# An RWKV block on one core: a planned order of work, with side-by-side spreads, one pool of PSUM banks, regrouped mixes, a deviation by quarters and joint norm scalars

## The chip, the cores and the metric

The kernel runs on one core of a Trainium2 chip. The metric is the time of one execution in device microseconds (us); lower is better. A core has five engines that run side by side, each through its own instructions in order: TensorE (PE) for matrix products, VectorE (DVE), ScalarE (ACT) and GpSimd (POOL) for work on elements, and SyncE (SP), which here issues nearly all transfers (DMA). Each engine waits at an instruction until what it needs is there, and all that stands behind it on that engine waits too.

## The reference

All numbers are fp32: 8 sequences (batches), 256 tokens, 512 channels, 32 heads of 16 channels. Cut to what matters:

```python
xn = ln(x, ln1_w, ln1_b);  sx = shift(xn) - xn
xxx = tanh((xn + sx * maa_x) @ maa_w1).reshape(b, l, 5, 1, 32)
xxx = matmul(xxx, maa_w2)                          # five mix groups
x5 = xn[:, :, None] + sx[:, :, None] * (maa_stack + xxx)
w = exp(-exp(time_decay + tanh(x5[1] @ decay_w1) @ decay_w2))
r, k, v = x5[3] @ Wr.T, x5[0] @ Wk.T, x5[2] @ Wv.T
g = silu(x5[4] @ Wg.T)
def step(s, r, k, v, w):                           # per head, state s is 16 x 16
    a = k[:, None] * v[None, :]
    return a + w[:, None] * s, r @ (faaaa * a + s)
att = scan(step)                                   # over the 256 tokens
att = group_norm(att) * gn_w + gn_b                # over 16 channels of a head
x = x + att * g @ Wo.T
xn2 = ln(x, ln2_w, ln2_b)                          # a second shift and a gated FFN
x = x + sigmoid(xr @ ffn_Wr.T) * (square(relu(xk @ ffn_Wk.T)) @ ffn_Wv.T)
```

`x5[g]` stands for group g of the five; `xk` and `xr` are two more mixes of `xn2` with its shift.

## The kernel before, in words

Channels lie on the 128 partitions in four blocks; a tile of shape [128, 2, 256] holds two blocks (a half, q = 0 or 1) by 256 tokens. For each of the eight batches three stages are recorded.

`inputs_of_scan` (L588) loads x, norms it (`normed`, L491: statistics on DVE at L499 and L500, three small POOL instructions per tile of 128 tokens at L501 to L503, scaling on ACT at L505, transposition on PE at L517), forms the shift on POOL (L526) and the first mix (L537, L539), and makes the small product that feeds the five groups (L595, L582, tanh into the tile `ta`). `mixed` (L606) makes groups: a "lot" of four matmuls that contract over 32 rows each (L620), an add-and-multiply on DVE for each block (L629), an add on POOL (L631). It is called for groups (1, 0), then (2, 3), then (4,). Then come the decay (L582, L640, L650, L657) and the projections k, v, r and g (L552 and ACT copies at L665, L675).

`scan` (L677): for each of four blocks, v goes through DRAM (`vo`, issued by ACT at L712) and comes back four times as `vs`, repeated so that each partition has one of a head's 16 rows (the DMA recorded at L726). ACT writes the first column (L728), DVE multiplies by k (L731; `kp` is a copy of k in PSUM) and runs the recurrence as one scan of 1,024 elements (L733), POOL multiplies by r (L736). When four of these are done, PE sums over the rows (`gather`, L744, into the PSUM tile `pat`) and DVE adds the result to `att` (L750). The term with faaaa is formed once for each batch (L687, L692) as `c`, with one row for a group of channels, and is spread over the partitions by eight small DMAs for each half (`att<-c`, L705); POOL multiplies it by v (L707). DMAs that `dma` records all carry line 380 in the profile.

`rest` (L756): squares (L762), their mean over a head (L770, four matmuls into column strips of 32), square root (L775), reciprocal on DVE (L777, 256 elements wide). In seven batches the result is spread by eight small DMAs for each half (L799) and POOL multiplies (L801); in the last, PE spreads it (L785) and DVE multiplies (L793). Then the scale of the group norm (L805), the product with g (L807), the output product (`project_tokens`, L567), the second norm, and the FFN with its three products (L552, L567). The weights Wo, ffn_Wk, ffn_Wr and ffn_Wv are loaded anew for each batch into eight tiles `Ws`.

The order of all instructions is made when the program is built, by the class `Plan`. Each piece of work is recorded with its engine, a cost in us, what it writes and what it reads. `TURNS` gives each piece a rank (a list written out by hand, one number for each piece of each stage). `order` (L281) takes pieces that can start, lowest rank first, gives them a start time from the recorded costs, latencies and free buffers, and the program is emitted by start time. Buffers come from named pools; a piece takes a buffer when it is placed, and the buffer comes free when the last piece that names it is done. The costs in the plan are therefore part of what sets the order. In PSUM there are eight banks: two for `wrep`, two for `kp`, one for `pat`, three for `ps` (all other products). `mix` has eight tiles, `vs` five.

The recorder lets a piece that writes a tile wait for the last writer and all readers of that tile. In the plan, the eight spreads into one tile are therefore one after the other, each with the recorded DMA latency:

```python
LATENCY = {"PE": 0.25, "DVE": 0.12, "ACT": 0.2, "POOL": 0.15, "DMA": 2.6}
def dma(out, in_, dst, kb, src=None):
    plan.add("DMA", 0.05 + kb / 300, ...)
```

Of the kernel before, what the change touches and what calls it, by code (L numbers as in the profile page):

```python
# [12 lines left out]
P = 128  # L13
# [18 lines left out]
C_SUM = C_MEAN + 32  # L32
# [4 lines left out]
class Buf:  # L37


    def __init__(self, pool, name, view=lambda t: t):  # L40
        self.pool, self.name, self.place, self.left, self.view = pool, name, None, 0, view
        self.writer, self.readers, self.until = None, [], 0.0
        self.first = self.last = None
# [14 lines left out]
class Plan:  # L58
# [4 lines left out]
    LATENCY = {"PE": 0.25, "DVE": 0.12, "ACT": 0.2, "POOL": 0.15, "DMA": 2.6}  # L63
    SWITCH = {"ACT": 1.3, "PE": 0.1}

# [12 lines left out]
    def add(self, engine, us, outs, ins, emit, mode=None, into=(), lag=0.0):  # L78
        op = Op(engine, us, outs, ins, emit, mode)
        op.lag = self.LATENCY[engine] + lag  # L80
# [4 lines left out]
        for b in ins:  # L85
            edges.add(b.writer)
            b.readers.append(op)
        for b in outs:
            edges.add(b.writer)
            edges.update(b.readers)  # L90
            b.writer, b.readers = op, []
        for o in edges - {None, op}:
            op.before.append(o)
            o.after.append(op)
        self.stages[-1].append(op)

    def stage(self):
# [6 lines left out]
        388 1540 181 998 1450 2523 1312 1981 2661 297 2571 1221 1131 2433 2751 711 2162 4536 2071 1620 2857 3167  # L104
        3186 3205 414 621 531 440 207 971 1019 1205 1064 1112 1459 1157 1376 1668 1283 1331 1401,
        0 90 350 420 450 472 530 564 441 510 549 571 629 663 822 973 991 1047 1119 767 847 865 921 993 1263 1311
        1375 1113 1161 1225 1495 1681 1931 1971 2000 2359 2481 2524 2576 2564 2607 3421 2055 2177 2257 2309 2217
        2297 2681 2706 2826 2855 2883 2912 3106 3228 3803 3272 3510 3575 3921 4119 5076 5252 5450 2576 2698 2777
        2863 2738 2817 2968 2879 3001 3044 3096 3084 3127 3201 3226 3402 3600 3748 4440 4869 4094 4613 4811 4267
        4786 4984 4969 5164 5365 5416 5124 5204 5256 6788 7016 7298 6109 6285 6630,  # L110
        817 908 1168 1237 1579 1601 1659 1726 1258 1328 1480 1502 1560 1594 1830 2025 2044 2111 3526 2194 2274 2292
        2348 2420 3711 3759 3823 2540 3848 5127 5425 5611 5731 5771 5799 6468 6602 6802 7476 6642 6842 6957 5855
        5977 6057 6226 6017 6338 6852 7816 7975 8004 8033 8082 9245 9367 9414 9759 9806 8137 8313 8595 7189 7545
        7917 8005 8178 8258 8536 8218 8298 8746 7438 7674 7754 8058 7714 7914 8641 8713 8889 9087 10184 10711 10909
        9525 9701 9899 9062 9352 9550 9884 10076 10500 10552 10036 10236 10405 11001 11177 12506 11874 12120 12448,
        1710 1891 2060 2130 2786 2808 3325 3359 2337 2407 3306 3344 3402 3436 6961 7227 7245 7356 8430 5962 6089
        6127 6183 7062 8551 8653 10300 7182 7408 8851 10420 10606 10726 10765 10794 11360 11732 11812 12909 11532
        11692 11798 10894 11148 11268 11693 11109 11228 11480 13203 13499 13528 13557 13585 14239 14361 14408 14453
        15185 12329 12505 12703 12795 12971 13184 12688 13101 13181 13252 13061 13141 13412 13308 13485 13685 13920
        13445 13524 13576 14056 14346 14751 14519 14695 14893 15260 15436 15634 13707 13883 14081 15120 15303 15567  # L120
        16084 15263 15951 16266 16386 16562 16946 17149 17325 17651,
# [818 lines left out]
```

## Time and profile before

| what | value |
|---|---|
| three timed runs | 699.48, 701.94, 705.77 us; median 701.94 |
| the profiled execution | 702.79 us, of it a span of 701.0 |
| granted TensorE clock, mean | 0.978 |
| busy: PE, DVE, POOL, ACT | 649.5, 570.3, 539.2, 347.0 us |
| DMA | 132.09 MB, mean 188 GB/s |
| scan on DVE (L733), 128 times | 2278 ns each |
| multiply by k on DVE (L731), 128 times | 1206 ns each |
| multiply by r on POOL (L736), 128 times | 2000 ns each |
| reciprocal on DVE (L777), 8 times | 1743 ns each |
| first `vs` multiply; last gather's end | 48.25 us; 647.0 us |
| `vs<-vo`, issue to landing, median | 5.6 us, 512 KB read out each |
| `att<-c`, `rk<-sq`, `sq<-sq`, issue to landing | 4.0, 4.0 and 3.7 us |

How to read it: a row of the costliest groups gives line, engine, operation, what is written and read with sizes, the count, busy us and mean ns, and then the idle time of that engine just before those instructions with what ended it. `PE ... x8` counts records: an fp32 matmul leaves two. PE's busy time counts a matmul that runs at a lower granted clock as longer. Releasers are inferred. A wait of an engine costs time only where that engine, or what waits for it, sets the end.

### The profile page before, as it was taken

Reading aid. Unit: us, or ns where it says so; the run is one execution under the profiler, and the core shown is the slowest. Engines: PE = TensorE matmul, PEld = TensorE weight load, DVE = VectorE, ACT = ScalarE, POOL = GpSimd, SP = SyncE. Lnnn points to the kernel's source line nnn. Section 1 sums busy time; section 2 is a strip of 40 time slices with the busy share of each in tenths; the row PEclk is TensorE's granted clock in tenths of the full one; section 3 lists DMA queues with packets and bytes.
Section 4 is the critical chain, followed back from the end, with each engine's and each line's share of the span. In section 5 each row is a group of like instructions: output and inputs, shape, how many; then the busy total and the mean of one; then the engine's idle time right before and its main releaser. Section 6 shows DMA issues by size and latency. Waiting matters only on the chain.

```text
span 701.0 us, 10714 instructions
## 1 busy us (share of the span) xinstructions
PE 649.5 (93%) x3688; PEld 429.8 (61%) x3688; DVE 570.3 (81%) x567; ACT 347.0 (50%) x716; POOL 539.2 (77%) x474
## 2 busy tenths in 40 slices
PE   5799999899899899999999999999999999698997
PEld 4487676675646486557764686577756676345453
DVE  2539999999999999889898889899797999896310
ACT  5244542543882467425582368246753365463450
POOL 4528789688898998688978799698877988679151
PEclk9699999999999999999999999999999999999999
DMA  8778754757879669865987669968787658983442
GB/s 269 229 184 212 170 137 114 188 147 189 206 198 243 181 144 243 216 184 162 237 217 198 179 177 230 242 174 222 180 210 181 161 157 200 233 226 114 142 152 89
DMA packets 65415, 132.09 MB, mean 188 GB/s; under 512 B 11281, under 2 KB 24081, under 8 KB 65361
## 3 DMA queue, kind: packets, MB, share of 16 engines
q1 hardware_dynamic: 60752, 127.21, 69.8%
q10 hardware_dynamic: 4608, 4.20, 2.0%
q8 instruction: 29, 0.48, 0.3%
q14 instruction: 26, 0.20, 0.1%
HBM read 115.11 MB, written 8.39 MB: 176 GB/s over the span
## 4 chain that ended last, share of the span: by engine, by line
PE 39%; DVE 11%; DMA 10%; issue 5%; ACT 2%; POOL 2%; SPq 2%; POOLq 0%; DVEq 0%; ACTq 0%
PE ps L567 15%; PE ps L552 14%; DMA vs<-vo 7%; DVE st L733 5%; PE pat L744 4%; DVE vs L731 3%; PE ps L620 3%; SPq L380 2%; DMA att<-c 1%; PE ps L582 1%; DMA s<-in_state 1%; DMA Ws<-in_wo 1%; PE ps L517 1%; PE ps L595 1%; DVE mix L629 1%
## 5 line engine op out<-in xcount | busy, mean ns | idle before, releaser
L733 DVE TENSOR_TENSOR_SCAN st<-wrep,vs 128x1024 f32<-128x1024 f32 x128 | 289.5, 2278 | 7.8 <-PE pat L744 2.6
L736 POOL TENSOR_TENSOR st<-st,r 128x1024 f32<-128x1024 f32 x128 | 255.1, 2000 | 43.1 <-DVE st L733 32.7
L731 DVE TENSOR_TENSOR vs<-vs,kp 128x1024 f32<-128x1024 f32 x128 | 152.9, 1206 | 20.5 <-ACT vs L728 20.3
L567 PE MATMUL ps<-Ws,mix 128*128 128x512 f32 x256 | 119.1, 612 | 6.7 <-DMA Ws<-in_fr 4.3
L631 POOL TENSOR_TENSOR mix<-mix,xn 128x512 f32<-128x512 f32 x80 | 86.5, 1090 | 32.0 <-DVE mix L629 31.8
L728 ACT ACTIVATE vs<-s,cm 128x4 f32<-128x4 f32 x128 | 36.8, 296 | 116.7 <-DMA vs<-vo 113.6
L567 PEld LDWEIGHTS ps<-Ws,mix 128*128 128x128 f32 x256 | 48.3, 195 | 64.5 <-issue 56.4
L629 DVE SCALAR_TENSOR_TENSOR mix<-ps,vec,sx 128x256 f32<-128x256 f32 x160 | 67.8, 474 | 12.6 <-PE ps L620 11.6
L744 PE MATMUL pat<-st,con 128*32 128x256 f32 x1024 | 64.0, 386 | 6.0 <-DVE att L750 5.8
L552 PE MATMUL ps<-mix,Wg 128*128 128x256 f32 x256 | 62.9, 397 | 0.9 <-DVE mix L629 0.9
L552 PE MATMUL ps<-mix,Ws 128*128 128x256 f32 x256 | 58.0, 382 | 4.6 <-ACT vs L728 1.9
L552 PE MATMUL ps<-mix,Wv 128*128 128x256 f32 x256 | 61.7, 392 | 0.0
L552 PE MATMUL ps<-mix,Wk 128*128 128x256 f32 x256 | 59.9, 384 | 1.4 <-ACT sq L775 0.8
L552 PE MATMUL ps<-mix,Wr 128*128 128x256 f32 x256 | 59.2, 382 | 1.2 <-POOL mix L631 0.8
L552 PEld LDWEIGHTS ps<-mix,Wg 128*128 128x128 f32 x256 | 49.0, 197 | 14.8 <-issue 5.0
L567 PE MATMUL ps<-Ws,g 128*128 128x512 f32 x128 | 56.9, 596 | 0.7 <-POOL g L807 0.7
L552 PEld LDWEIGHTS ps<-mix,Ws 128*128 128x128 f32 x256 | 47.9, 190 | 13.6 <-POOL mix L539 4.9
L539 POOL TENSOR_TENSOR mix<-mix,xn 128x512 f32<-128x512 f32 x48 | 51.6, 1091 | 5.9 <-ACT mix L537 5.7
L552 PEld LDWEIGHTS ps<-mix,Wk 128*128 128x128 f32 x256 | 47.6, 190 | 13.2 <-issue 4.6
L552 PEld LDWEIGHTS ps<-mix,Wv 128*128 128x128 f32 x256 | 48.7, 195 | 10.7 <-issue 3.2
L552 PEld LDWEIGHTS ps<-mix,Wr 128*128 128x128 f32 x256 | 47.9, 190 | 10.4 <-issue 1.9
L744 PEld LDWEIGHTS pat<-st,con 128*32 128x32 f32 x1024 | 31.1, 110 | 34.9 <-DVE att L750 9.4
(82 smaller groups left out, 815.4 us busy)
## 6 DMA issues: line engine op xcount, KB each, us to landing
vs<-vo SPq DMA_DIRECT2D x128, 512.0 KB, 5.6
Ws<-in_wo SPq DMA_DIRECT2D x32, 256.0 KB, 5.0
Ws<-in_fv SPq DMA_DIRECT2D x32, 256.0 KB, 4.0
Ws<-in_fk SPq DMA_DIRECT2D x32, 256.0 KB, 4.0
Ws<-in_fr SPq DMA_DIRECT2D x32, 256.0 KB, 4.7
xt<-in_x SPq DMA_DIRECT2D x16, 256.0 KB, 3.1
x<-in_x SPq DMA_DIRECT2D x16, 256.0 KB, 5.0
vo<-v ACTq DMA_DIRECT2D x32, 128.0 KB, 3.8
```

The source lines that it names most:

```text
L380: plan.add("DMA", 0.05 + kb / 300, [out] if out else [], [src] if src else [], lambda: nc.sync.dma_start(out=dst(), in_=in_()))
L539: gp(512, t, [t, xn[q]], lambda q=q, t=t: nc.gpsimd.tensor_tensor(t(), t(), xn[q]()[:, :, 1 : T + 1], ALU.add), 1.8)
L552: nc.tensor.matmul(ps()[:, m, :], lhsT=w[k]()[:, o : o + P], rhs=src[k // 2]()[:, k % 2, :], start=(k == 0), stop=(k == NK - 1),)
L567: nc.tensor.matmul(ps().rearrange("p m t -> p (m t)"), lhsT=src[h]()[:, k % 2, n * P : (n + 1) * P], rhs=w[k](), start=(k == 0), stop=(k = ...
L620: nc.tensor.matmul(ps[g, q]()[:, m, :], lhsT=w2()[lo : lo + MAA, k * P : (k + 1) * P], rhs=ta()[lo : lo + MAA, i, :], start=True, stop=True,)
L629: dve(256, [t], [p_, vec, sx[q]], lambda g=g, q=q, m=m, t=t, p_=p_: nc.vector.scalar_tensor_tensor(t()[:, m, :], p_()[:, m, :], col(f"maa_ ...
L631: gp(512, t, [t, xn[q]], lambda q=q, t=t: nc.gpsimd.tensor_tensor(t(), t(), xn[q]()[:, :, 1 : T + 1], ALU.add), 1.8)
L728: act(4, vs, [s0, cm], lambda i=i, blk=blk, vs=vs: nc.scalar.activation(vs()[:, :, 0:1], s0()[:, blk, 4 * i : 4 * i + 4].rearrange("p (n o ...
L731: dve(4 * T, [vs], [vs, kp], lambda m=m, vs=vs, kp=kp: nc.vector.tensor_tensor(vs(), vs(), kp()[:, m : m + 1, :].to_broadcast([P, 4, T]), ...
L733: dve(4 * T, [st], [w, vs], lambda w=w, vs=vs, st=st: nc.vector.tensor_tensor_scan(st().rearrange("p n t -> p (n t)"), w().rearrange("p n ...
L736: gp(4 * T, st, [st, r], lambda m=m, st=st, r=r: nc.gpsimd.tensor_tensor(st(), st(), r()[:, m : m + 1, :].to_broadcast([P, 4, T]), ALU.mult))
L744: nc.tensor.matmul(pat()[32 * i : 32 * i + 32, 0, :], lhsT=con()[:, s : s + 32], rhs=done[i]()[:, j, :], start=(j == 0), stop=(j == 3),)
```

## The change

Seven things are changed together.

- In the plan, the parts of a spread (pieces that write parts of one tile) no longer wait for each other (`part=True`); a tile keeps a list of writers.
- The plan's prices: an issued DMA holds SP for 0.6 and then a shared wire for kb/270; the latencies, a gap between dependent pieces of one engine (`GAP`), and the costs of ACT, DVE and POOL pieces have other numbers.
- PSUM: `kp`, `pat` and `ps` become one pool of six banks. `mix` has 12 tiles instead of 8, `vs` 6 instead of 5. A setting of the program (`dynamic_dma_scratch_size=1024`) is added.
- `mixed` is called for groups (1, 0, 2) and (3, 4): lots of six and of four matmuls.
- In all batches but the last, the mean of squares is laid out by quarters of the tokens: sixteen matmuls of 64 columns fill all 128 rows of a tile 64 wide. Square root and reciprocal run on 64 elements, one DMA writes the result to DRAM (`dev`), and the spreads read it from there.
- The norm's scalars of both token tiles are made together: two POOL instructions and one DVE instruction for a norm, in place of six on POOL.
- L707 and L807 have their operands the other way round, and all of `TURNS` is new.

```diff
-    LATENCY = {"PE": 0.25, "DVE": 0.12, "ACT": 0.2, "POOL": 0.15, "DMA": 2.6}
+    LATENCY = {"PE": 0.3, "DVE": 0.18, "ACT": 0.16, "POOL": 0.12, "DMA": 1.1}
+    GAP = {"PE": 0.03, "DVE": 0.16, "ACT": 0.04, "POOL": 0.11, "DMA": 0.03}
...
-            edges.add(b.writer)
-            edges.update(b.readers)
-            b.writer, b.readers = op, []
+            if not part or b.readers or not b.writers or b.writers[0].engine != engine:
+                b.before = {*b.writers, *b.readers}
+                b.writers, b.readers = [], []
+            edges.update(b.before)
+            b.writers.append(op)
...
-            free[op.engine] = op.end
+            free[op.engine] = landed = op.end
+            if op.wire:
+                wire = landed = max(wire, op.end) + op.wire
...
-        plan.add("DMA", 0.05 + kb / 300, [out] if out else [], [src] if src else [], lambda: nc.sync.dma_start(out=dst(), in_=in_()))
+        plan.add("DMA", 0.6, [out] if out else [], [src] if src else [], lambda: nc.sync.dma_start(out=dst(), in_=in_()),
+                 lag=lag, kb=kb, part=part)
...
-    pool("mix", 8, [P, 2, T])
+    pool("mix", 12, [P, 2, T])
...
+    pool("dev", 2, [H, T], dram)
-    pool("vs", 5, [P, 4, T])
+    pool("vs", 6, [P, 4, T])
...
-    pool("kp", 2, [P, 2, T], pp)
-    pool("pat", 1, [P, 2, T], pp)
-    pool("ps", 3, [P, 2, T], pp)
+    pool("ps", 6, [P, 2, T], pp)
...
-            gp(1, rs, [mv, eh], each=60, emit=lambda rs=rs, mv=mv: nc.gpsimd.tensor_tensor(rs(), mv()[:, 1:2], eh()[:, 0:1], ALU.add))
-            gp(1, rs, [rs, eh], lambda rs=rs: nc.gpsimd.tensor_tensor(rs(), rs(), eh()[:, 1:2], ALU.pow), 420)
-            gp(1, nm, [mv, rs], lambda nm=nm, mv=mv, rs=rs: nc.gpsimd.tensor_scalar(
-                nm(), mv()[:, 0:1], rs(), -1.0, ALU.mult, ALU.mult), 60)
+        gp(2, rs, [mv, eh], lambda: nc.gpsimd.tensor_tensor(rs(), mv()[:, :, 1], eh()[:, 0:2], ALU.add), 30)
+        gp(2, rs, [rs, eh], lambda: nc.gpsimd.tensor_tensor(rs(), rs(), eh()[:, 2:4], ALU.pow), 250)
+        dve(2, [nm], [mv, rs], lambda: nc.vector.scalar_tensor_tensor(
+            nm(), mv()[:, :, 0], -1.0, rs(), ALU.mult, ALU.mult))
...
-            if len(pair) == 2:
-                lots = [[(pair[0], q, w2a, pair[0], 0), (pair[1], q, w2a, pair[1], 0)] for q in range(NQ)]
-            else:
-                lots = [[(4, q, w2b, q, 1) for q in range(NQ)]]
+            lots = [[(g, q, w2b, 0, 1) if g == 4 else (g, q, w2a, g, 0) for g in pair] for q in range(NQ)]
...
-        x5 = mixed((1, 0))
+        x5 = mixed((1, 0, 2))
...
-        x5.update(mixed((2, 3)))
+        x5.update(mixed((3, 4)))
...
-        x5.update(mixed((4,)))
...
-                    att(), att(), v()[:, :, 1 : T + 1], ALU.mult), 1.85)
+                    att(), v()[:, :, 1 : T + 1], att(), ALU.mult))
...
+        parts = 1 if b == NB - 1 else 4
+        nt, c = T // parts, C_MEAN if parts == 1 else C_QUA
...
+                for i in range(parts):
+                    at = blk % 2 * T + nt * i
+                    nc.tensor.matmul(
+                        pv()[32 * blk : 32 * blk + 32, 0, 0:nt], lhsT=con()[:, c + 32 * i : c + 32 * i + 32],
+                        rhs=sqs[blk // 2]()[:, at : at + nt], start=(i == 0), stop=(i == parts - 1))
...
+        dve(nt, [rs], [rs], lambda: nc.vector.reciprocal(rs()[:, 0:nt], rs()[:, 0:nt]), 6.25)
+        if parts > 1:
+            dev = new("dev", f"dev{b}")
+            dma(dev, lambda: rs()[:, 0:nt], lambda: dev().rearrange("h (u t) -> (h u) t", u=parts), 32, rs, 0.8)
...
-                        dma(rsb, lambda blk=2 * q + n: rs()[32 * blk : 32 * blk + 32, 0:T],
-                            lambda n=n, rows=rows, rsb=rsb: by_block(rsb)[rows, n, :], 32, rs)
+                        dma(rsb, lambda blk=2 * q + n: dev()[HB * blk : HB * blk + HB, :].unsqueeze(1).to_broadcast([HB, 4, T]),
+                            lambda n=n, rows=rows, rsb=rsb: by_block(rsb)[rows, n, :], 32, dev, 0.8, True)
...
-            gp(512, g, [g, att], lambda g=g, att=att: nc.gpsimd.tensor_tensor(g(), g(), att(), ALU.mult))
+            gp(512, g, [g, att], lambda g=g, att=att: nc.gpsimd.tensor_tensor(g(), att(), g(), ALU.mult))
```

In the changed kernel the lines of the prediction's steps stand at L590 (mix lots), L700 and L702 (multiply and scan), L713 (gather), L743 (mean of squares), L750 (reciprocal), and DMAs at L351.

## The prediction, made before the result

> **What bounds the kernel now.** I read the page first, then a table of stretches, the waits by engine, and the chain of waits in order of time.
>
> ```profile
> span 701.0 us, 10714 instructions
> PE 649.5 (93%) x3688; PEld 429.8 (61%) x3688; DVE 570.3 (81%) x567; ACT 347.0 (50%) x716; POOL 539.2 (77%) x474
> PE   5799999899899899999999999999999999698997
> DVE  2539999999999999889898889899797999896310
> PEclk9699999999999999999999999999999999999999
> ```
>
> PE is the fullest engine, but DVE stands at 9 through the first third. The table of stretches shows the two limits apart (busy us of PE, PEld, DVE, ACT, POOL; granted clock; DMA share):
>
> ```profile
> 20.00:30.00 10.00, 6.50 (x38) 4.21 (x36) 6.87 (x17) 1.55 (x4) 5.51 (x7) 0.57 0.98 319
> 30.00:40.00 10.00, 8.92 (x31) 6.47 (x32) 3.88 (x8) 3.67 (x9) 6.89 (x10) 0.58 0.23 67
> 180.00:200.00 20.00, 17.31 (x119) 12.10 (x118) 19.52 (x17) 17.91 (x40) 18.73 (x16) 1.00 0.86 225
> 400.00:420.00 20.00, 20.00 (x122) 16.43 (x115) 16.67 (x16) 12.25 (x28) 16.57 (x17) 1.00 0.62 167
> 580.00:600.00 20.00, 15.59 (x89) 11.38 (x88) 17.75 (x11) 10.23 (x20) 14.99 (x11) 1.00 0.86 217
> 600.00:620.00 20.00, 16.09 (x65) 8.64 (x66) 16.93 (x13) 9.21 (x16) 14.04 (x10) 0.83 0.90 212
> ```
>
> From 20 to 40 us PE waits and then runs at 0.57 of its clock. From 50 to 280 us DVE is busy for 220.4 of 230, and PE waits for it. From 280 to 580 PE is full and DVE waits. From 580 to 620 both wait: 8.3 us of PE idle, and 3.4 us (20 x 0.17) to a lower clock. After 647 only PE's closing work is left.
>
> ```profile
> ACT vs L728 <- DMA vs<-vo: 113.6, 50, 6.2
> DVE vs L731 <- ACT vs L728: 20.3, 13, 5.6
> PE ps L567 <- DMA Ws<-in_fr: 4.3, 1, 4.3
> SPq L380 <- DVE st L733: 96.1, 45, 5.9
> ```
>
> The scan's inputs (vs) come by DMA through a free vs buffer; ACT puts in the first column and DVE follows. DVE loses 20.3 us there, and the 4.3 us of PE in the 580 stretch is a weight load that was issued late, among spreads.
>
> ```profile
> 397.09 1.73 PE ps L552 x8
> 398.82 1.06 PE ps L620 x8
> 399.88 1.86 PE pat L744 x32
> 401.75 1.93 PE ps L552 x8
> ```
>
> This piece of the chain prices PE: eight records (four matmuls of 256 columns) take 1.73 us, and 0.20 more when PE comes from another tiling (pat) to them; a lot of four 32-row matmuls (L620) takes 1.06; sixteen 32-column matmuls, four side by side, 1.86.
>
> **The sum's base.** The profiled execution took 702.79 us (span 701.0 and 1.8 around it), 0.85 above the median 701.94. I change 702.8 and take 0.85 off.
>
> **Mix groups three and two.** 40 lots of L620 become 32; the 160 matmuls stay, 16 lots hold three groups and 16 two. If the third row group runs beside the others as the fourth column group does in L744, a lot stays at 1.06: 8 x 1.06 = 8.5 us off PE. If only two run side by side, a lot of three costs 0.43 more: 16 x 0.43 gives 6.8 back, 1.6 off. I take -7.8, near the first, because L744 is the row with more than two side by side.
>
> **Deviation by quarters.** The matmuls of line 770 (eight records in 0.64 us at 512.28) become 32 records of 64 columns for seven batches. They are written block by block, so four in a row go to the same column strip. Least: 0.64, as now, the same columns in all. Most: the sixteen-record, 128-column row of L582 (1.02 us, 0.064 a record) gives 32 x 0.064 = 2.05. I take 1.0 more each, +7 (0 to +9.9). On DVE the reciprocal (1.743 us, L777) runs on a quarter of the elements: 0.44 to 0.5, seven times, -8.7. On ACT the square root gets shorter, which hides. On SP, seven more DMAs, and the spreads must now wait until the copy in DRAM has landed: the small spreads land in 3.8 us (median), vo in DRAM also in 3.8, and SP issues one in 0.59. In six of the seven batches the first spread stands right behind that copy in SP's order, so all behind it, vs loads and weights, wait too.
>
> The Trainium skill, "TensorEngine Tiling", section Performance Considerations, speaks against the quarters: a matmul carries about 60 cycles of overhead, and a dimension that is already small should not be tiled further. No row here has 64 columns; an estimate from that page puts the price at the upper end, 2.9 us of PE more than I take, of which 1.8 would fall in the PE-bound part: a forecast near 686.
>
> **PE's changes of tiling.** In the two built orders they go from 177 to 163: 14 x 0.19 = -2.7. PE in all: -7.8 + 7 - 2.7 = -3.5 (-11.2 to +5.6).
>
> **Joint norm scalars.** Each norm drops six POOL instructions (2 x (189 + 549 + 265) ns = 2.0 us) for two (0.19, and 0.55 to 1.1 for the power), and gives DVE one small instruction, 0.18 by L500: POOL loses 0.7 to 1.3 a norm, about 16 in all, under DVE's and PE's cover; DVE 16 x 0.18 = +2.9. Both tiles must now be in before either is scaled; that costs only where no other matmul is queued, the tail. Swapping the operands of L707 and L807 can change POOL by 0.18 and 0.09 each against the 1.09 us of its kin, 16 times: -4.4 to +4.4, covered by DVE and PE as the rest.
>
> **Six shared banks, 12 mix, 6 vs buffers; new turns.** The order moves all engines' instructions, but not the balance: summed over my rows, PE's work ahead of the 16th gather is the same within 2 us, ahead of the 28th 3 us less. So I cost the new order by stage.
>
> Head: at 22.91 the second lot waits 2.54 us for DVE to empty a bank, the third 0.96, then 1.08 more at 33.02; all at the low clock. Six banks let the first six groups go in one piece. DVE needs 12 x 0.415 = 5.0 us for them and POOL 6 x 1.09, so v can start some 4 us earlier than at 35.03, and with it the first scan (48.25). SP's loads before the first vs are 36 as against 42. -4 (0 to -7, if the copies of x that stand ahead of vs on SP come as late as now, or not).
>
> DVE-bound, 48 to 280: three reciprocals 3.7 less, five norms 0.9 more: -2.8. Of the 9.6 us of DVE idle here the sixth vs buffer and the free pat bank take a quarter: -2.2. Together -5 (0 to -12).
>
> PE-bound, 280 to 640: five eighths of -3.5: -2 (-7 to +3.5). PE idle and clock loss from 280 to 620 are 13.9 + 5.2 = 19.1 us (the clock: 1.8 at 0.91 from 360 to 380, 3.4 from 600), 11.7 of it the stretch from 580 to 620, where SP issues two dozen spreads one by one between vs and weight loads. The planner now prices such an issue at 0.6, near its row (0.59; it had 0.16), so a plan made by it should not walk into that. I take less than half, -8 (0, if new stalls of that size come, to -18). What comes late next is vs behind a run of spreads.
>
> Tail, after the last gather: 40 token matmuls as before, one more fk group of 1.73 to fill; the joint scalars wait for the second tile (0.69 + 0.69), and the two matmuls left after the transposes cover 1.7 us where four covered 3.5: +1 (0 to +3).
>
> Sum: -4 - 5 - 2 - 8 + 1 = -18: 702.8 - 18 = 684.8, less 0.85: 684 us.
>
> **Rivals.** Slower: SP. In the after order the longest runs of other DMAs between two vs loads are 21, 21, 21, 19 and 19; before 17, 17, 15 and 14 (the loads at the start left out). 21 x 0.59 + 3.8 of standing = 16.2 us. Six vs buffers last 6 x (1.21 + 2.28) = 20.9 us of scan, less 5.6 for the next landing: 15.3. It is short by 0.9 where DVE has only scan work. If the copy lands at the upper end of its rows (6.0, so 2.2 later) and the next vs 1.2 above its median (its rows reach 12.3), it is short by 4.3: seven batches, 30 us, 714 us. It decides from 3.6 us a batch ((709 - 684)/7). For it: 113.6 us of ACT's waits are for vs. Against it: DVE has other work between scans (570 us for 128 scans is 4.5 us each, not 3.5), which stretches the cover by 6 us.
>
> The Trainium skill, "DMA: Bandwidth & Descriptors", section Anatomy of one DMA, puts about 2.0 us of fixed time on a DMA of the software path, most of it the receipt from the target memory, heaviest for HBM. Our vo row has 3.8 on a hardware queue, and the measurement decides; with 2.0 the run would last 14.4 and this rival would vanish, the forecast staying at 684.
>
> No change: the edits do what they say on paper, but the third group does not run beside the others, the quarters cost the most, and the new turns have stalls as large as the old: five eighths of 9.1 and the 8 come back: 684 + 6 + 8 = 698. For it: the balance of the order hardly moves. Against: 8.3 us of PE's idle stands in one stretch with one cause, spreads priced too low in the plan.
>
> More gain: banks and vs buffers end most waits between 48 and 640: -12 in the DVE part, -18 in the PE part: 684 - 7 - 10 = 667. Against: full buffers only help where a buffer was the last to come.
>
> **How the numbers follow.** Forecast 0.46 (671 to 695), more gain 0.17, no change 0.18, SP 0.19. Measuring this kernel cannot tell less than about 1% (7 us) from nothing. Faster 0.63, within 1% 0.18, slower 0.19. The range 664 to 712 leaves out the better half of the best case and the worse half of the SP case; the likeliest case alone has 671 to 695.
>
> **What would show it.** Right: line 590's lots of three at about 1.1 us; DVE reciprocals near 0.5; the first scan before 46 us; no stretch after 50 us with more than 3 us of PE idle in 20; granted clock over 0.98. Wrong: line 743 over 1.7 us a batch; DVE waiting for ACT vs over 25 us in all, behind SP waiting for dev; PE idle of 8 us in one stretch.

## The result, and the profile after

The changed kernel takes 723.22 us (median; 719.36 to 724.22), the kernel before 702.64 us on the same chip: a ratio of 1.028, interval [1.023, 1.033]. It is slower by 2.8%; 684 us were forecast, with 712 as the upper end. The profiled execution of the changed kernel took 719.36 us, its span is 717.6, 16.6 us over the span before.

The page of the changed kernel, its busy times, slices and the chain by engine and by line:

```profile
span 717.6 us, 11006 instructions
PE 646.2 (90%) x3856; PEld 432.9 (60%) x3856; DVE 570.1 (79%) x583; ACT 345.5 (48%) x718; POOL 518.2 (72%) x410
PE   5899799988998898999989999998899898879987
PEclk9999999999999999999999999999999999989999
PE 29%; DMA 18%; DVE 14%; issue 8%; ACT 7%; SPq 6%; POOL 4%; ACTq 1%; POOLq 0%; DVEq 0%
```

PE has 3.3 us less to do than before and still ends 16.6 later: its idle time rose from 51.5 to 71.4 us. SP's queue holds 6% of the chain; it held 2%. The table of stretches (columns as in the prediction):

```profile
20.00:30.00 10.00, 7.76 (x52) 5.74 (x47) 7.81 (x21) 5.02 (x12) 8.52 (x10) 0.83 0.86 303
30.00:40.00 10.00, 10.00 (x53) 8.03 (x53) 5.49 (x12) 5.72 (x13) 7.02 (x7) 1.00 0.61 157
580.00:600.00 20.00, 19.40 (x147) 15.92 (x146) 15.94 (x13) 11.35 (x25) 13.28 (x11) 1.00 0.89 199
600.00:620.00 20.00, 17.30 (x87) 12.02 (x86) 17.00 (x11) 10.66 (x21) 16.34 (x11) 0.91 0.76 194
620.00:640.00 20.00, 13.61 (x54) 5.78 (x53) 15.99 (x13) 10.57 (x16) 13.59 (x9) 0.83 0.68 168
```

The head is better, as meant: no slow clock from 30 to 40 us. The hole of 580 to 620 has moved to 600 to 640. The waits, of all engines and then of SP's own queue (in one execution: total us, times, longest us):

```profile
DVE vs L700 <- ACT vs L697: 29.7, 22, 4.6
DVE nm L474 <- POOL rs L473: 9.7, 9, 1.6
PE ps L540 <- DMA Ws<-in_wo: 6.2, 3, 3.4
PE ps L540 <- DMA Ws<-in_fv: 3.9, 2, 3.0
PE ps L540 <- DMA Ws<-in_fr: 2.3, 1, 2.3
```

```profile
SPq L351 <- DVE st L702: 86.5, 34, 9.1
SPq L351 <- DMA vo<-v: 63.8, 12, 9.9
SPq L351 <- DMA dev<-sq: 23.4, 6, 5.1
```

DVE waits 9.4 us more for vs than before, PE 12.4 us for weights in these rows (before: 4.3 + 1.1), and SP has a new row: 23.4 us behind the copy to DRAM. The timeline of SP in the fourth batch shows that row as it comes about:

```profile
355.98 0.55 SPq L351 DMA_DIRECT2D vs<-vo  x1
356.62 0.53 SPq L351 DMA_DIRECT2D dev<-sq  x1
361.01 1.43 SPq L351 DMA_DIRECT2D rk<-dev  x2
...
373.01 0.66 SPq L351 DMA_DIRECT2D rk<-dev  x1
373.77 0.39 SPq L351 DMA_DIRECT2D Ws<-in_fv  x1
374.27 2.48 SPq L351 DMA_DIRECT2D vs<-vo  x4
```

The copy is issued at 356.62, the first spread at 361.01, the last ends at 373.67: SP is taken for 17.1 us, 4.4 of it from the copy's issue to the first spread, and a spread takes 0.65 to 0.7 us to issue (0.59 before). Four vs loads and the last part of ffn_Wv wait behind.

Where the time went can be read from the start of the first scan of each batch in DVE's timeline, and of the last scan of all (one execution each, in us):

| kernel | batch 0 | 1 | 2 | 3 | 4 | 5 | 6 | 7 | last scan | end |
|---|---|---|---|---|---|---|---|---|---|---|
| before | 49.5 | 118.1 | 189.5 | 260.9 | 342.0 | 418.4 | 498.8 | 575.6 | 638.5 | 701.0 |
| after | 41.5 | 111.6 | 183.1 | 259.4 | 340.4 | 422.9 | 508.4 | 591.4 | 654.4 | 717.6 |
| after, without the copy (e1_direct) | 43.1 | 111.9 | 181.4 | 254.6 | 336.1 | 416.1 | 498.2 | 574.3 | 634.9 | 696.4 |

The change gains 8.0 us in the head, keeps 6.4 of it to batch 2, and then loses 22 us from batch 2 to the last scan. The tail loses 0.7.

### The profile page after: what moved, and what is told of

Its sections match the earlier page's. It is cut to its first block, busy times and chain, and to the rows that moved or that the text cites. A ratio compares the mean times of both kernels' runs of the same rounds, so it can differ in the third digit from the quotient of the medians.

```text
span 717.6 us, 11006 instructions
## 1 busy us (share of the span) xinstructions
PE 646.2 (90%) x3856; PEld 432.9 (60%) x3856; DVE 570.1 (79%) x583; ACT 345.5 (48%) x718; POOL 518.2 (72%) x410
## 4 chain that ended last, share of the span: by engine, by line
PE 29%; DMA 18%; DVE 14%; issue 8%; ACT 7%; SPq 6%; POOL 4%; ACTq 1%; POOLq 0%; DVEq 0%
PE ps L540 14%; DMA vs<-vo 11%; PE ps L525 8%; DVE st L702 7%; SPq L351 6%; DVE vs L700 4%; PE ps L713 3%; DMA Ws<-in_wo 2%; DMA att<-c 2%; PE ps L590 1%; DVE mix L599 1%; ACT mix L510 1%; DMA dev<-sq 1%; POOL st L705 1%; ACT xh L478 1%
## 5 line engine op out<-in xcount | busy, mean ns | idle before, releaser
L702 DVE TENSOR_TENSOR_SCAN st<-wrep,vs 128x1024 f32<-128x1024 f32 x128 | 288.7, 2280 | 12.7 <-ACT wrep L687 5.7
L700 DVE TENSOR_TENSOR vs<-vs,ps 128x1024 f32<-128x1024 f32 x128 | 152.6, 1209 | 30.1 <-ACT vs L697 29.7
L540 PE MATMUL ps<-Ws,g 128*128 128x512 f32 x128 | 63.3, 649 | 14.5 <-POOL g L783 8.2
L713 PE MATMUL ps<-st,con 128*32 128x256 f32 x1024 | 66.3, 397 | 7.4 <-POOL st L705 4.6
L599 DVE SCALAR_TENSOR_TENSOR mix<-ps,vec,sx 128x256 f32<-128x256 f32 x160 | 65.5, 477 | 9.2 <-PE ps L590 9.1
L525 PE MATMUL ps<-mix,Ws 128*128 128x256 f32 x256 | 59.8, 389 | 4.2 <-POOL mix L512 3.9
L525 PE MATMUL ps<-mix,Wg 128*128 128x256 f32 x256 | 59.2, 384 | 3.0 <-ACT mix L798 2.8
L525 PEld LDWEIGHTS ps<-mix,Wv 128*128 128x128 f32 x256 | 49.5, 197 | 10.0 <-issue 2.3
L713 PEld LDWEIGHTS ps<-st,con 128*32 128x32 f32 x1024 | 32.2, 113 | 38.4 <-issue 11.9
L540 PEld LDWEIGHTS ps<-Ws,g 128*128 128x128 f32 x128 | 25.8, 206 | 48.1 <-issue 32.5
```

The costliest lines, as they stand in the source:

```text
L525: nc.tensor.matmul(ps()[:, m, :], lhsT=w[k]()[:, o : o + P], rhs=src[k // 2]()[:, k % 2, :], start=(k == 0), stop=(k == NK - 1),)
L540: nc.tensor.matmul(ps().rearrange("p m t -> p (m t)"), lhsT=src[h]()[:, k % 2, n * P : (n + 1) * P], rhs=w[k](), start=(k == 0), stop=(k = ...
L599: dve(256, [t], [p_, vec, sx[q]], lambda g=g, q=q, m=m, t=t, p_=p_: nc.vector.scalar_tensor_tensor(t()[:, m, :], p_()[:, m, :], col(f"maa_ ...
L700: dve(4 * T, [vs], [vs, kp], lambda m=m, vs=vs, kp=kp: nc.vector.tensor_tensor(vs(), vs(), kp()[:, m : m + 1, :].to_broadcast([P, 4, T]), ...
L702: dve(4 * T, [st], [w, vs], lambda w=w, vs=vs, st=st: nc.vector.tensor_tensor_scan(st().rearrange("p n t -> p (n t)"), w().rearrange("p n ...
L713: nc.tensor.matmul(pat()[32 * i : 32 * i + 32, 0, :], lhsT=con()[:, s : s + 32], rhs=done[i]()[:, j, :], start=(j == 0), stop=(j == 3),)
```

## The experiments

All ratios are to the kernel before on the same chip, with their 95% intervals. Theories at the start: S, SP's standing for the copy costs the time; N, DVE's new wait for POOL's power does; T, the new turns do.

**Without the copy.** e1_direct: the deviation runs 256 wide and the spreads read it from SBUF, as before; turns and order stay.

```diff
-        parts = 1 if b == NB - 1 else 4
+        parts, spread = 1, b < NB - 1
...
-            dma(dev, lambda: rs()[:, 0:nt], lambda: dev().rearrange(...), 32, rs, 0.8)
...
-            dma(rsb, lambda blk=2 * q + n: dev()[HB * blk : HB * blk + HB, :].unsqueeze(1).to_broadcast([HB, 4, T]),
+            dma(rsb, lambda blk=2 * q + n: dev()[32 * blk : 32 * blk + 32, :],
```

> The after kernel with its own turns and the same order on every engine; only the deviation goes back to full width (four matmuls, a reciprocal of 256 elements) and the spreads read it from SBUF, without the copy to DRAM. SP no longer stands for the copy (23.4 us in six waits in the after trace), DVE has 7 x 1.2 = 8.5 us more work, PE 7 x 0.68 = 4.8 us less. Theory S, the stand on SP is the cause: vs and weights come earlier, DVE and PE stalls shrink, 705 to 714 us. Theory T, the new turns follow a plan that the chip does not keep, and each late piece holds up its engine's queue: the waits move elsewhere, 717 to 727 us.

Measured: 1.000 [0.997, 1.003]. Its waits for vs and, by PE, for the batch's weights (2.0 us in all) are those of a kernel that is not held up:

```profile
DVE vs L700 <- ACT vs L697: 20.1, 18, 3.0
```

The whole loss goes, more than S had asked for.

**The norm's scalars.** e2_nm_pool: nm by two POOL instructions again.

```diff
-        dve(2, [nm], [mv, rs], lambda: nc.vector.scalar_tensor_tensor(nm(), mv()[:, :, 0], -1.0, rs(), ...
+        dve(2, [nm], [mv, rs], lambda: [nc.gpsimd.tensor_scalar(
+            nm()[:, n : n + 1], mv()[:, n, 0:1], rs()[:, n : n + 1], -1.0, ALU.mult, ALU.mult) for n in range(NT)])
```

> The after kernel in the same order; only the last scalar of the joint norm is made by POOL (two instructions of 0.265 us) in place of one on DVE, so that DVE no longer stands for POOL's power (9.7 us of DVE waits and 16 x 0.3 us of busy time in the after trace). Theory N, this wait is the cause of the loss: 710 to 714 us. Theories S and T: most of those waits lie beside others, 719 to 724 us.

Measured: 1.032 [1.030, 1.035]. N falls: the instruction with 9.7 us of waits and 7.7 us of work left DVE, and nothing was gained.

**The turns.** e4_old_turns: all edits, with the ranks of the kernel before carried over to the new pieces. e5_old_turns_both: the same with the edits of e1_direct and e2_nm_pool.

> All edits of the after kernel (prices, side-by-side spreads, six shared banks, 12 mix and 6 vs buffers, lots of three and two, quarters through DRAM, joint norm with the DVE scalar), but with the ranks of the kernel before, carried over piece by piece; a lot takes the rank of its first group, and the added group's pieces come right behind their mates. Theory T: the loss goes away with the new turns, 692 to 705 us. Theory S or N: the DRAM hop and the DVE wait are still there, 712 us or more.

> As the kernel with old ranks and all edits, but with the deviation at full width spread from SBUF and the norm's last scalar on POOL: lots, banks, buffers, side-by-side spreads and two instead of six POOL instructions for rs are left. Theory T: 690 to 703 us, and no more than 5 us from the run with all edits and old ranks. Theory S or N: 10 us or more below that run.

Measured: 1.060 [1.054, 1.066] and 1.042 [1.039, 1.044]. T falls as put: the edits do worse with the old ranks. The old ranks were made for other pools, so this does not say how good the new ones are. Taking out the copy (and N) gains 14 us here too.

**Both edits on the new turns.** e3_both: e1_direct with the edit of e2_nm_pool.

> The changed kernel with the direct spread and with nm made by two POOL instructions; same turns. Candidate to beat both. The direct spread alone gave 1.0; DVE loses 9.4 us of waits for POOL's power and 7.7 us of work there. If DVE's work bounds the first half, 4 to 8 us come of it: 0.985 to 0.995. If those waits only stand beside others (as in the changed kernel itself, where the same edit moved nothing), 0.995 to 1.005.

Measured: 1.002 [0.999, 1.005]. No gain: DVE's scalars stand beside other waits.

**Stand, issues or quarters?** f1_wide_hop keeps the copy and drops the quarters (128 KB go to DRAM, 32 rows of it into each spread). f2_stale keeps everything but reads the deviation of the batch before, so that only the stand goes.

```diff
 f1_wide_hop
-    pool("dev", 2, [H, T], dram)
+    pool("dev", 2, [P, T], dram)
...
-            dma(dev, lambda: rs()[:, 0:nt], lambda: dev().rearrange("h (u t) -> (h u) t", u=parts), 32, rs, 0.8)
+            dma(dev, lambda: rs()[:, 0:nt], lambda: dev(), 32, rs, 0.8)
...
-  ... lambda blk=2 * q + n: dev()[HB * blk : HB * blk + HB, :].unsqueeze(1).to_broadcast([HB, 4, T]),
+  ... lambda blk=2 * q + n: dev()[32 * blk : 32 * blk + 32, :],
 f2_stale
+    pool("old", 7, [H, T], dram)
...
-  ... lambda blk=2 * q + n: dev()[HB * blk : ...
+  ... lambda blk=2 * q + n: old[max(b - 1, 0)][HB * blk : ...
```

> The changed kernel with the copy through DRAM kept, but without the quarters: deviation, square root and reciprocal run 256 wide, 128 KB go to DRAM, and the spreads read them there; same plan and same turns. Theory S (SP stands until the copy has landed): against the direct spread (ratio 1.0 to before) only the copy is put back, so the 26 us come back; 1.02 to 1.04 of before, and SP waits for dev 20 us or more in all. Rival Q (the quarters' 32 small matmuls and their place in PE's order cost the time): without them it stays at the direct spread's time, 0.99 to 1.01.

> The changed kernel with the same orders and all its transfers, but the spreads of batch b read the deviation of batch b-1, which has long been in DRAM (the output is not the reference's; only batch 0 reads its own). Only the stand of SP behind the copy goes. Theory S: nearly all of the loss goes with it, 0.985 to 1.01 of before; SP waits for dev once. Rival H (the hop costs by what else it brings: reads from DRAM instead of SBUF, 0.65 instead of 0.59 us for an issue, sixteen in a row, quarters on PE): it stays at 1.02 or more.

Measured: 0.998 [0.994, 1.002] and 1.001 [0.998, 1.005]. So S as put falls: in f1_wide_hop SP still stands 20 us behind the copy, and it costs nothing.

```profile
SPq L351 <- DMA dev<-sq: 20.0, 6, 5.3
```

What differs there is the issue. SP's timeline of f1_wide_hop, first batch:

```profile
128.48 0.34 SPq L351 DMA_DIRECT2D dev<-sq  x1
131.63 0.34 SPq L351 DMA_DIRECT2D rk<-dev  x1
132.07 0.36 SPq L351 DMA_DIRECT2D sq<-dev  x1
...
135.72 1.81 SPq L351 DMA_DIRECT2D sq<-dev  x4
```

A spread that reads 32 rows of DRAM once takes 0.34 to 0.45 us here (102 of 112 take no longer), one that reads eight rows four times over 0.65. Theory C follows: what counts is how long SP is taken from the copy to the last spread. g1_wide_bcast tests it: f1_wide_hop, but each spread reads eight rows four times over, as in the changed kernel (the values are the same).

```diff
-  ... lambda blk=2 * q + n: dev()[32 * blk : 32 * blk + 32, :],
+  ... lambda blk=2 * q + n: dev().rearrange("(h r) t -> h r t", r=4)[HB * blk : HB * blk + HB, 0, :].unsqueeze(1).to_broadcast([HB, 4, T]),
```

> The kernel with the wide copy through DRAM (0.998 of before), with one thing put back from the changed kernel: each spread reads eight rows of the DRAM copy four times over instead of 32 rows once (the same values), so that SP takes 0.65 us for an issue instead of 0.42. No quarters; all orders as in the changed kernel. Theory C (what counts is SP's whole run from the copy to the last spread, stand plus sixteen issues: 15.6 to 20.4 us in the changed kernel; 11.3 to 13.4 in the batches with few other transfers between, in the kernels that ran as fast as before): the run is as long as the changed kernel's again, 1.018 to 1.033. Rival Q (the quarters' matmuls, or what they do to PE's order, are the other half): 0.995 to 1.007.

Measured: 1.029 [1.024, 1.034]. C holds on this order and Q (quarters) falls. SP's time from the copy (without one: the first spread) to the end of the last spread, mean of batches 2 to 5, where at most three other transfers lie between:

| kernel | SP taken | PE waits for wo, fk, fr, fv | ratio |
|---|---|---|---|
| e1_direct | 11.4 us | 2.0 us | 1.000 |
| f1_wide_hop | 12.4 | 1.9 | 0.998 |
| f2_stale | 12.8 | 1.6 | 1.001 |
| after | 16.5 | 12.4 | 1.028 |
| g1_wide_bcast | 16.7 | 12.6 | 1.029 |

Up to 1.4 us more than 11.4 cost nothing; 5.1 and 5.3 more cost 20 us in all. They do not cost it in every batch. The first scans of f2_stale stand at 43.3, 112.9, 185.3, 258.4, 340.9, 418.4, 499.7 and 576.4 us, the last at 639.2: up to 340 us the changed kernel is at most 1.0 us behind, though its copies of the second and third batch keep SP 2.6 and 3.6 us longer; then it is behind by 4.5, 8.7 and 15.0 us. So the copies of the fourth, fifth and sixth batch cost 4 to 6 us each, and the earlier ones, in the stretch where DVE is full, nothing that shows. g1_wide_bcast beside f1_wide_hop gives the same picture; beside e1_direct 4.8 us are lost by the fourth batch. These are single executions, so the split is less sure than the sum.

**The copy on the kernel before.** f3_before_hop: the quarters through DRAM; f3b_before_wide_hop: the wide copy alone. The order of before is untouched.

```diff
+        def inverse():
+            nc.vector.reciprocal(rs()[:, 0:nt], rs()[:, 0:nt])
+            if parts > 1:
+                nc.sync.dma_start(out=dev.rearrange("h (u t) -> (h u) t", u=parts), in_=rs()[:, 0:nt])
...
-        dve(256, [rs], [rs], lambda: nc.vector.reciprocal(rs()[:, 0:T], rs()[:, 0:T]), 6.25)
+        dve(256, [rs], [rs], inverse, 6.25)
```

> The kernel before, with the deviation by quarters through DRAM as its one change; its turns, plan and prices are untouched, the copy is issued right behind the reciprocal. Theory S: the stand comes here too (about 4 us less one or two transfers that lie between the copy and the first spread, seven times, part of it hidden): PE +4.8 for the quarters, DVE -8.5, stand +7 to +20: 1.01 to 1.03 of before. Rival T (the copy is harmless where the spreads are interleaved with loads; it needs the new turns with sixteen spreads in a row): 0.99 to 1.007.

> The kernel before with the copy through DRAM alone, 256 wide and without quarters, its order untouched. The stand is added (3.3 to 4 us a batch), and sixteen issues become 0.17 us shorter each (2.7 us). Theory C: the two nearly cancel, 0.998 to 1.012. Rival Q: 0.995 to 1.005, as the quarters are not there. A rival that the stand alone costs it (because the loads between the spreads are held up by all of it): 1.015 to 1.03, as the quarters through DRAM gave on the kernel before (1.031).

Measured: 1.031 [1.025, 1.038] and 1.016 [1.011, 1.020]. The copy does its harm without the new turns; that the shorter issues would pay for the stand was wrong here, where the spreads lie among loads and all of these stand too. It also bounds C: by the table's measure f3b_before_wide_hop takes SP for 20.6 us and the kernel before for 20.4, with 13 to 17 other transfers in each run, and yet it is 1.6% slower. SP's time as measured in the table tells the loss only where the spreads stand together. PE's wait for weights shows 5.1 us of f3b_before_wide_hop's loss (10.5 against 5.4 in all rows):

```profile
PE ps L568 <- DMA Ws<-in_fr: 7.5, 1, 7.5
PE ps L568 <- DMA Ws<-in_fv: 3.0, 1, 3.0
```

**Who behind SP pays?** Four things wait behind the run: vs, the spread tile itself, weights, and the next spreads. Each of the next kernels frees one of the first three, on the changed kernel and without moving anything else.

g3_fifo7: seven vs tiles handed out in turn. h1_vs_ahead: the same, and one vs load a batch moved ahead of the copy.

```diff
+        for c in [op for op in done if op.engine == "DMA" and op.bufs[0].pool == "dev"]:
+            at = done.index(c)
+            for op in [op for op in done[at:] if op.engine == "DMA" and op.bufs[0].pool == "vs"][:1]:
+                ...
+                    done.remove(op)
+                    done.insert(done.index(c), op)
```

> The changed kernel, quarters, copy and all orders kept, with one vs buffer more: the plan still reckons with six, so that no instruction moves, and the vs tiles are then handed out in turn among seven. Theory C: the seventh buffer covers one scan and multiply more (3.5 to 4.5 us) of SP's run, which is 4 to 5 us too long: 0.995 to 1.012 of before. Rival (the run costs through weights or att that come late, not through vs; or the quarters themselves): 1.02 to 1.03, as the changed kernel.

> The changed kernel with its copy and quarters and seven vs tiles in turn, and in each of the seven batches the first vs load that stood behind the copy on SP's queue moved ahead of it; nothing else moves. Theory V (SP's long run costs by the vs loads that come late behind it): one more load in hand covers 3.5 of the 4 to 5 us a batch by which the run is too long, so most of the loss goes, 1.000 to 1.014 of before. Theory A (it costs by the spread tile itself, which is complete 5 us later, and with it the output product, the second norm and the FFN): 1.022 to 1.035.

h2_no_wait_att: POOL's product reads g in place of the spread.

```diff
-                    att(), att(), by_block(rsb), ALU.mult))
+                    att(), att(), g(), ALU.mult))
```

> The changed kernel with all its instructions and transfers in the same order, but POOL's product after the spreads reads the gate tile g, long there, instead of the spread deviation (so the deviation is not applied, and the output is not the reference's); nobody waits for the spreads' data any more. Theory A: most of the loss goes, 0.99 to 1.012 of before. Theory V: nearly all of it stays, 1.02 to 1.03.

w1_weights_ahead: three weight loads a batch moved ahead of the copy (as in h1_vs_ahead), eleven Ws tiles. w3_no_wait_weights: the products read the gate's weights.

```diff
-  ... lhsT=src[h]()[:, k % 2, n * P : (n + 1) * P], rhs=w[k](),
+  ... lhsT=src[h]()[:, k % 2, n * P : (n + 1) * P], rhs=W["g"][k](),
```

> The changed kernel with its copy, quarters and vs loads, and in each of the seven batches the first three weight loads that stood behind the copy on SP's queue moved ahead of it, into eleven Ws tiles handed out in turn instead of eight; nothing else moves. Theory W (the run on SP costs by the weight loads behind it: TensorE waits 12.4 us for them in the changed kernel, 10.5 to 15.1 in all kernels at 1.0155 or above that keep the copy, 2.0 or less in those at 1.00): most of the loss goes, 1.000 to 1.015 of before, and PE waits for weights under 5 us. Rival D (everything behind the run is late together, so that freeing one sort of load leaves the next): 1.02 to 1.035, as moving vs ahead gave.

> The changed kernel with all its instructions and transfers in the same order, but the output product and the FFN's products read the gate's weights, which stay on the core, instead of the loaded ones (so these products are not the reference's, and neither is the output); nobody waits for the loaded weights, and SP no longer waits for TensorE before it loads over them. Theory W: most of the loss goes, 0.99 to 1.012 of before. Rival D: 1.018 to 1.03.

Measured: g3_fifo7 1.030 [1.025, 1.034], h1_vs_ahead 1.034 [1.029, 1.040], h2_no_wait_att 1.028 [1.022, 1.034], w1_weights_ahead 1.028 [1.022, 1.035], w3_no_wait_weights 1.020 [1.012, 1.028]. With seven vs tiles SP waits less for a free one (24.8 us for a scan instead of 86.5 in g3_fifo7), but a load that stands behind the run stays behind it, and DVE waits for vs as long as it did (30.0 us, 29.7 in the changed kernel). h1_vs_ahead did not free vs alone: a load of 512 KB ahead of the copy lengthened SP's run to 17.9 us, from 16.5. The orders of the changed kernel and of f2_stale are the same on every engine, so their timelines can be laid beside each other. The lag grows at PE's products with loaded weights: 15.2 of 17.8 us. After, and then f2_stale, the same eight records in the fourth batch:

```profile
373.04 1.10 PE L540 MATMUL ps<-Ws,mix 128*128 128x512 f32 x2 [0.98 <-DMA Ws<-in_fv]
377.10 4.54 PE L540 MATMUL ps<-Ws,mix 128*128 128x512 f32 x6 [2.97 <-DMA Ws<-in_fv]
```

```profile
372.71 3.70 PE L541 MATMUL ps<-Ws,mix 128*128 128x512 f32 x8 [0.19 <-DVE mix L600]
```

3.95 us of waiting, and 5.64 us for eight records where f2_stale needs 3.70. The slower records go with a lower granted clock (third from the right): 0.62 over the six behind the second wait, 1.00 in f2_stale:

```profile
377.10:381.64 4.54, 4.54 (x9) 1.72 (x9) 0.43 (x1) 0.30 (x1) 4.54 (x6) 0.62 1.03 226
372.71:376.41 3.70, 3.70 (x11) 1.51 (x11) 3.70 (x9) 1.15 (x2) 3.65 (x4) 1.00 1.03 235
```

And yet freeing these loads entirely (w3_no_wait_weights) wins back about a third, 0.009 of 0.028, and not even that for certain, as the intervals overlap. Another wait grows in its place, DVE's for vs from 29.7 to 39.6 us:

```profile
DVE vs L700 <- ACT vs L697: 39.6, 28, 6.6
```

In w1_weights_ahead PE still waits 9.2 us for weights instead of 12.4, and SP's run is as long as it was (17.1 us by the measure of the table). The spread tile (h2_no_wait_att) and the weights (w3_no_wait_weights) were freed wholly, and neither alone is the cause; vs was never freed wholly. That what stands behind the run is late together, so that freeing one leaves the next, fits all of these runs; it is not shown, as no run freed two at once. Only making SP's run shorter, by the stand or by the issues, took the loss away, and making it as long again (g1_wide_bcast) brought it back.

**Where the rest of the forecast stayed.** e1_direct has no loss by SP and still no gain. g4_direct_fifo7 gives it seven vs tiles, h4_direct_ahead also a vs load ahead of the spreads, h6_lots_undone issues the third group's matmuls behind the pair's.

```diff
-                    for m in range(2):
-                        for g, q, w2, row, i in lot:
+                    for m, (g, q, w2, row, i) in [(m, x) for part in (lot[0:2], lot[2:]) for m in range(2) for x in part]:
```

> The changed kernel with the direct spread (no copy, deviation 256 wide; 1.0 of before) and seven vs tiles handed out in turn, no instruction moved. Candidate to beat both. If vs supply still bounds it (its chain is 13% vs transfers, and DVE waits 20 us for vs): 0.97 to 0.99. If the six were enough once the stand is gone: 0.995 to 1.003.

> The kernel with the direct spread and seven vs tiles (0.9994 of before), with one vs load a batch moved ahead of the spreads as well. Candidate to beat both. Theory V, with the vs loads behind the spreads still too late now and then (the batches from the fourth on lose the head's 6 us): 0.985 to 0.995. If the vs loads are early enough once the stand is gone: 0.996 to 1.003.

> The kernel with the direct spread (1.0 of before), with the third group's matmuls of each lot behind the pair's instead of among them: two row groups side by side, then one; no instruction leaves its piece of the plan. It puts back about 16 x 0.45 = 7 us on PE. If PE's work sets the pace once the stand is gone: 1.006 to 1.010. If the saved PE time only became idle time elsewhere (PE idle 59.0 us against 51.5 before): 0.997 to 1.004.

Measured: 0.999 [0.997, 1.002], 1.001 [0.997, 1.004] and 1.000 [0.996, 1.003]. More vs in hand does not help once the stand is gone. h6_lots_undone put no work back: PE was busy with the lots for 35.4 us against 36.1 in e1_direct, so the third row group runs beside the others in that order too, and the question it asked stays open. No kernel of the study beats the kernel before by more than the measurement tells.

## Why the prediction was wrong, step by step

- **The copy on SP**: the failed step. 39 us lie between 684 and 723: about 20 by which the copy made the kernel slower than before, and the forecast gain, which does not come without the stand either (f2_stale, with all other edits: 1.001). The text said that in six batches the first spread stands right behind the copy and that all behind it waits too, but the sum has no term for it; it was left to the rival SP, at 0.19 and 714 us. From the copy's issue to the first spread 3.8 to 5.8 us passed in those six batches (3.8 taken), and 0.59 for an issue was the row of a spread that reads SBUF; reading eight rows of DRAM four times over takes 0.65 to 0.7. The rival reckoned that vs would run out, with 6 us of cover by DVE's other work against it. Neither is what the runs show: they show 20 us in all at 16.5 us of SP, nothing at 12.8, and vs is only one of several that are late. So the rival had the place, with 30 us where 20 were measured, by a mechanism too narrow; that its 714 came nearer than the forecast is in part luck, since it was reckoned from 684, and the gain to 684 never came.
- **PE-bound part, -10** (-2 and -8): e1_direct, free of the stand, lost 2.7 us against before from batch 3 to the last scan (380.3 against 377.6), the changed kernel 17.4. The holes that were to give 8 us were not closed but moved: in that stretch PE's idle time and its loss to a lower clock are 28.0 us in e1_direct, 20.1 before. One wait stands out there, for the product behind the spreads of the seventh batch, and the eight records behind it run at a granted clock of 0.56:

```profile
611.83 6.51 PE L540 MATMUL ps<-Ws,g 128*128 128x512 f32 x8 [6.56 <-POOL g L784]
611.83:618.34 6.51, 6.51 (x9) 2.88 (x10) 6.01 (x3) 0.54 (x2) 6.29 (x4) 0.56 0.46 120
```

  "A plan made by it should not walk into that" failed: the plan's price of an issue was right, but for the copy it reckons with 2.6 us from issue to landing (0.6, 0.1 of wire, 1.1 + 0.8), and 3.8 to 5.8 passed.
- **DVE-bound part, -5**: from batch 0 to batch 3 the changed kernel needs 217.9 us, before 211.4, e1_direct 211.5. The reciprocals fell as reckoned (534 ns against 1743), and nm takes 161 ns in the median, near the 180 reckoned, but six of the sixteen take 452 to 1,860 ns (mean 482), and DVE waits 9.7 us in all before it; e2_nm_pool and e3_both show that this slack moves nothing by itself. f1_wide_hop, level with before in time, also needs 217.4 us here, so these 6.5 us do not go with the loss.
- **PE in all, -3.5**: measured -3.3, but by cancelling. The groups, by form, after:

```profile
L590 PE MATMUL ps<-ta,mw2a 32*128 32x256 f32 x256 | 34.4, 398 | 6.4 <-ACT w L627 3.4 <-ACT ta L576 1.8 <-DVE mix L599 0.5
L474 DVE SCALAR_TENSOR_TENSOR nm<-mv,rs 128x2 f32<-128x2 f32 x16 | 7.7, 482 | 9.7 <-POOL rs L473 9.7
L743 PE MATMUL ps<-sq,con 128*32 128x64 f32 x224 | 9.9, 222 | 0.6 <-DVE att L719 0.6
L750 DVE RECIPROCAL sq<-sq 128x64 f32<-128x64 f32 x7 | 3.7, 534 | 0.0
```

  The mix lots took 48.9 us before and 35.0 now, both weights' lots together: -13.9 instead of -7.8, since the third row group costs nothing (a lot of three groups by itself takes 1.14 us, one of two 1.13; 1.10 in the mean of all) and the lots before had taken 1.22 in the mean, not the 1.06 of the one that was read: most took 1.13, those in the head at a granted clock of 0.5 up to 2.1. The quarters took 10.6 against 6.9: +3.7, not +7. Against these stands the output product (`ps<-Ws,g`), 63.3 us against 56.9 in the groups (649 ns a record against 596); it has the longest waits before it. 112 of its 128 records run at the full granted clock and take 597 ns; 16, behind such waits, run at 0.50 to 0.72 of it and take 1,015. Before, all 128 run at the full clock. That term was not in the sum. After, and then f2_stale's, the same eight records of the sixth batch, and the granted clock over the first row's (0.68):

```profile
560.89 5.37 PE L540 MATMUL ps<-Ws,g 128*128 128x512 f32 x8 [3.36 <-DMA Ws<-in_wo]
547.62 3.67 PE L541 MATMUL ps<-Ws,g 128*128 128x512 f32 x8 [0.47 <-DMA Ws<-in_wo]
560.89:566.26 5.37, 5.37 (x10) 2.07 (x10) 1.35 (x4) 0.00 (x0) 5.37 (x4) 0.68 0.67 151
```

- **The Trainium skill's page "TensorEngine Tiling (Array Packing)"**, section Performance Considerations, has about 60 cycles of overhead for a matmul. The prediction took that for the upper end of its range, 2.05 us a batch, but did not work the cycles out as a time; the 2.05 is from the row of L582. The row of the quarters has 1.41 (9.9 / 7), against 0.87 for the wide matmuls: 24 more records cost 0.54 us, about 23 ns each. The measurement decides against the upper end, not against the page.
- **The Trainium skill's page "DMA: Bandwidth & Descriptors"**, section Anatomy of one DMA, states its fixed 2.0 us for the software path; taken for SP's queue, as the prediction's estimate did, it would have made the rival vanish. The 3.8 to 5.8 us from the copy's issue to the first spread, on a hardware queue, are two to three times that, and the measurement decides. No run here shows the software path.
- **The head, -4**: right in sign, -8.0 measured, 1.0 past the end of its range (the text's 48.25 is the first multiply; the first scan of before starts at 49.5). **The tail, +1**: +0.7, right.
- **POOL**: 21.0 us less busy; forecast 16, with 4.4 either way for the swapped operands, which went the good way (1274 to 1094 ns, 1181 to 1089). Hidden, as said.
- **What would show it**: three of the five signs for "right" came (lots 1.10 us, reciprocals 0.53, first scan at 41.5); the clock (0.975) and the holes (6.4 us in 620 to 640) did not. Of those for "wrong" came DVE's wait for vs with SP's for dev behind it, and that one counted.

Open: why e1_direct, with 12.1 us less work on PE and a head 6.4 us shorter, ends level. PE's idle time there is 7.5 us longer (59.0 against 51.5), and from batch 1 on 77.1 us pass between first scans against 76.3. One place holds much of it: the wait of 6.56 us at 611.83, with eight records behind it that take 6.51 us instead of 3.67. POOL's product of the seventh batch waits there for its spreads, which lie among nine other transfers on SP; the same wait stands in the changed kernel (6.39) and in f2_stale (8.51). No run moved these spreads, so what it is worth stays open. More vs, POOL's scalars and the copy are excluded by runs; another order was not tried.

## What to carry to other kernels

A transfer that waits on an in-order queue holds up everything behind it. Before a round trip through DRAM goes onto the queue that also feeds the bottleneck, add up stand and issues in one piece and compare it with what is issued ahead, and put that sum into the forecast, not only into a rival. Price an issue from a row with the same source and shape. And where one wait is blamed, free it alone: here five runs aimed at one wait each, and none won back more than a third of the loss.

## What was not expected of the hardware

- A spread of 32 KB takes SP 0.34 to 0.45 us to issue when it reads 32 rows of DRAM, 0.59 from SBUF (the kernel before), and 0.65 when it reads eight rows four times over; the bytes are the same.
- Three row groups of 32 run side by side as cheaply as two (1.14 us against 1.13 for a lot), and do so even if the third's matmuls are issued behind the pair's (35.4 us for 32 lots).
- Swapping the operands of POOL's product went with 180 ns less of 1274 and 92 less of 1181; no run swapped them alone.
- DVE's product of two elements a partition (nm) takes 135 to 163 ns ten times and 452 to 1,860 ns six times; what holds up the six was not tried.
- Behind a wait of 3.36 us the same eight records took 5.37 us, at a granted clock of 0.68, that take 3.67 behind a wait of 0.47. A late transfer was paid for twice there.
